# Splitting the last undivided product of a Strassen-Winograd kernel, and letting VectorE and GpSimd share its sums by turns

## The chip, the cores and the metric

The kernel runs on one core of one Trainium2 chip. The core has a matrix engine (TensorE, PE in the profile; its weight loads are a row of their own, PEld), a vector engine (VectorE, DVE), a scalar engine (ScalarE, ACT), a general engine (GpSimd, POOL) and a queue that issues transfers (SyncE, SP). The metric is device time in microseconds (us) of one execution; smaller is better.

## The reference

Every one of 64 sequences of 64 tokens (width 1024, float32) passes two residual layers.

```
# layer 0: a low-rank adapter, chosen per sequence
x = x + (x @ B0[id0].T) @ A0[id0].T            # rank 16
# layer 1: a dense product, and a gated mixture of low-rank experts
logits = x @ Wr.T + 5.0 * one_hot(id1)          # 8 experts
gates  = softmax over the two largest logits, 0 elsewhere
y = x @ W.T + 2.0 * sum_e gates[e] * (x @ A1[e].T) @ B1[e].T
out = x + y
```

W is 1024 x 1024. That dense product over 4096 tokens is the bulk of the work, all of it in float32.

## The kernel before

**Tiling.** The data lie transposed: the width on 128 partitions in eight chunks, tokens along the free axis. Tokens come in eight blocks of 512. Two blocks make a super-block `s` (0 to 3), and in each super-block the dense product `(W + I) x` is one 2 x 2 block product in Winograd's form of Strassen's scheme: seven *outer* products `n`, run in `ORDER` 1, 2, 6, 7, 5, 3, 4, instead of eight. Each outer product is done in the same way again: seven *inner* products `k`, in which the weight tile is 256 x 256 and the tokens 256 wide. In super-blocks 1 to 3 some inner products are divided a third time into seven *fine* products of 128 x 128 weights and 128 tokens: `k = 2` always, `k = 4` for the `n` in `FOURTH`.

**What a division costs besides the matmuls.** A divided product needs sums and differences of the operands' quarters first, and its results must be added up after. Weight sums depend on W alone, so super-block 0 makes them and stores them in DRAM (`s_kept`, and `f_kept` for the fine ones, made in super-block 1); later super-blocks load them.

- `outer` (line 688) makes the four sums of W's quarters for the outer products 5, 7, 6, 3, on DVE.
- `weights` (line 709) makes in super-block 0, for every `n`, the four inner sums 5, 6, 7, 3 out of `n`'s quarters, on Pool, and stores all seven tiles with SP; later it loads them. Its tiles come from the pool of slots `"s"`, 27 of them.
- `fine_weights` (line 746) makes the four sums for a fine product (on Pool, one step) or loads them.
- `inner_tokens` (line 800) makes four differences of token quarters (`k` = 5, 6, 7, 4): on DVE in super-block 0, on Pool later. `begin_fine` (line 979) makes the tokens' sums for a fine product, on Pool, one step.
- `token_sum` (line 778) makes the outer sums of tokens, on DVE.
- `product` (line 918) issues the matmuls of an inner product: four calls of 256 columns, plus two where the expert term is added. A float32 call shows as two passes in the trace.
- `leave` (line 951) evacuates PSUM: a copy by ACT where nothing is to be added, otherwise an addition by DVE (PSUM plus an SBUF tile).
- `fine_product` (line 995) issues the fine matmuls in four parts. ACT copies the parts out (`copy`), and `rest_` adds them on Pool with three instructions.
- `whole_product` (line 889) is used for the pairs `(s, n)` in `WHOLE`, here only (0, 1): the outer product 1 of super-block 0 is not divided. It runs 4 x 4 calls of 512 columns, with four copies by ACT.

**The rest of the work.** Per block: the adapter of layer 0 (gathers of its rows by Pool, `turn`, `project`, `adapt`, whose results DVE adds to x), the rows of the experts (`rows`), the gates (`gates`: some twenty small DVE instructions in a chain), and `weigh`. In PSUM eight banks are given out as four "l", two "a" and two "b".

**The order.** Nothing is issued as written. Every step goes to `plan.add` with the engines that may run it and the time it is thought to take there, what it reads and writes, a due time `at` (one inner product is one unit, a super-block 49), the slots it takes, and `sb=True` where it reads SBUF with both operands. `Plan.order` (line 65) then plays the kernel through: again and again it takes the engine on which something can start first, and on it the step of lowest `at` among those within 0.2 us. The starts found order the instructions of each engine and each queue. Real waits are on data alone. Where steps marked `sb` run on DVE and Pool at once, `PACE` slows both in the plan (to 0.36 and 0.73 of their speed). This is the loop's core:

```
            e = min(can, key=lambda e: min(can[e]))
            t0 = min(can[e])[0]
            _, n, t = min((steps[n]["at"], n, t) for t, n in can[e] if t <= t0 + self.LOOK)
```

`products` (line 859) orders a super-block: `begin` adds the sums of an outer product one product ahead, `step` one inner product with its evacuation, and `advance` the next part of every fine product under way.

Of the kernel before, what the change touches and what calls it, by code (L numbers as in the profile page):

```python
# [14 lines left out]
P = 128  # L15
# [18 lines left out]
class Plan:  # L34
# [14 lines left out]
    AHEAD = 6.0  # L49
    PACE = {"DVE": 0.36, "POOL": 0.73}  # L50
    SET = {"SP": 1.2, "DVE": 3.1, "POOL": 2.9}

# [12 lines left out]
    def order(self):  # L65
# [34 lines left out]
        turn = {tag: 0 for tag in turns}  # L100
        clock, end, where, now = dict(self.SET), {}, {}, {}
        moved = 0.0
        done = []
# [4 lines left out]
        def start(n, e):  # L108
            st = steps[n]
            t = clock.get(e, 0.0)  # L110
            if st["kb"] and e == "SP":
                t = max(t, moved - self.AHEAD)
            for d in st["begun"]:
                t = max(t, steps[d]["start"] + 0.1)
            for d in st["dep"]:
                t = max(t, end[d] + (0.0 if where[d] == e and not steps[d]["kb"] else self.LAG))
            want = {}
            for tag, _ in st["take"]:
                want[tag] = want.get(tag, 0) + 1
            for tag, c in want.items():  # L120
                if len(free[tag]) < c or (tag not in self.shared and turns[tag][turn[tag]] != n):
                    return None
                t = max(t, sorted(free[tag])[c - 1] + self.LAG)
                if tag in self.shared:

                    for m in ready:
                        if sum(g == tag for g, _ in steps[m]["take"]) > c and steps[m]["at"] < st["at"] and data(m) <= t:
                            return None
            return t

        while ready:
# [7 lines left out]
            e = min(can, key=lambda e: min(can[e]))  # L139
            t0 = min(can[e])[0]  # L140
            _, n, t = min((steps[n]["at"], n, t) for t, n in can[e] if t <= t0 + self.LOOK)
            st = steps[n]
            ready.discard(n)
            clock[e] = t + st["eng"][e]
            other = {"DVE": "POOL", "POOL": "DVE"}.get(e)
            if st["sb"] and other in now and clock[other] > t and steps[now[other]]["sb"]:

                mine, theirs = st["eng"][e] / self.PACE[e], (clock[other] - t) / self.PACE[other]
                both = min(mine, theirs)
                clock[e] = t + both + (mine - both) * self.PACE[e]  # L150
                clock[other] = t + both + (theirs - both) * self.PACE[other]
                end[now[other]] = clock[other]
            now[e] = n
            end[n] = clock[e]
# [27 lines left out]
def kernel(  # L182
# [70 lines left out]

    WHOLE = {(0, 1)}

    FINE = 1
    FOURTH = (1, 2, 6, 7, 3)

    pe, dve = Pinned(tc, nc.tensor), Pinned(tc, nc.vector)
# [3 lines left out]
    slots = {  # L263
        "q": 7, "s": 27, "tt": 3, "cp": 3, "t5": 2, "t6": 2, "t7": 2, "t4": 2, "o": 3, "hg": 3, "hd": 3,
        "gb": 2, "ga": 1, "bt": 1, "bx": 1, "h": 1, "l": 4, "a": 2, "b": 2,
# [205 lines left out]
    def adapt(k, h, at):  # L471
# [33 lines left out]
        for gi in range(NG):  # L505
            xs = part(x, gs=[gi])
            plan.add({"DVE": 0.62}, out(gi), [(px[gi],)] + xs, xs, at - 2 + 1.5 * gi * (k == 0))

# [157 lines left out]
    s_kept = tc.dram_tile([7, 7, P, QC * QO], F32, name="s_kept")  # L666
    f_kept = tc.dram_tile([7, 2, P, QC * QO], F32, name="f_kept")

    def fine_of(s, n):

        return ((2, 4) if n in FOURTH and (s, n) != (NSUP - 1, ORDER[-1]) else (2,)) if s >= FINE else ()

# [11 lines left out]

    DVE = {"DVE": 0.62}
    POOL = {"POOL": 1.25}

    def outer(n, at):

        if n == 5:  # L690
            m_q[5] = {k: ("m5",) + k for k in quarter[1, 0]}
            for k in m_q[5]:
                combine(m_q[5][k], quarter[1, 0][k], quarter[1, 1][k], ALU.add, at, DVE)
        elif n == 7:
            m_q[7] = quarter[1, 0]
            for k in m_q[7]:
                combine(m_q[7][k], quarter[0, 0][k], m_q[7][k], ALU.subtract, at, DVE)
        elif n == 6:
            m_q[6] = quarter[0, 0]
            for k in m_q[6]:  # L700
                combine(m_q[6][k], m_q[5][k], m_q[6][k], ALU.subtract, at, DVE)
        elif n == 3:
            m_q[3] = quarter[0, 1]
            for k in m_q[3]:
                combine(m_q[3][k], m_q[3][k], m_q[6][k], ALU.subtract, at, DVE)

    wt, ti = {}, {}

    def weights(s, n, at):
# [17 lines left out]
        for k, (u, v, op) in {  # L727
# [7 lines left out]
            vv = m[v] if isinstance(v, tuple) else out[v]  # L735
            combine(out[k], uu, vv, op, at - 4, POOL)
        for k in ORDER:
# [8 lines left out]
    def fine_weights(s, n, k, a, at):  # L746

        t, kept = ("sf", s, n, k), f_kept[n - 1, k // 4]

        def blocks():  # L750
            made[t] = new("s", [P, QC, QO], f"sf_{s}_{n}{k}")
            return made[t].rearrange("p c (o w) -> p (c o) w", w=P)

# [3 lines left out]

        def sums(e):
            f, w4 = blocks(), made[a].rearrange("p c (o w) -> p (c o) w", w=P)
            a11, a21, a12, a22 = (w4[:, x] for x in range(4))  # L760
            v = engine[e]
            v.tensor_tensor(f[:, 0], a21, a22, ALU.add)
            v.tensor_tensor(f[:, 1], f[:, 0], a11, ALU.subtract)
            v.tensor_tensor(f[:, 2], a11, a21, ALU.subtract)
            v.tensor_tensor(f[:, 3], a12, f[:, 1], ALU.subtract)

# [3 lines left out]
        if s == FINE:  # L770
            plan.add({"POOL": 1.6}, sums, [(a,)], [(t,)], at - 3, [("s", t)], sb=True)
            plan.add({"SP": 0.1}, keep, [(t,)], [("fine", n, k)], at + 4, kb=256)
        else:
            plan.add({"SP": 0.1}, load, [("fine", n, k)], [(t,)], at - 6, [("s", t)], kb=256)
        wt[n]["fine", k] = t
# [24 lines left out]
    def inner_tokens(s, n, m, at):  # L800
# [7 lines left out]
        for k, u, v in ((5, (0, 1), (0, 0)), (6, (1, 1), 5), (7, (1, 1), (0, 1)), (4, (1, 0), 6)):  # L808
            t = ("ti", s, n, k)

            def fn(e, t=t, k=k, u=u, v=v):
# [5 lines left out]
            plan.add(  # L817
                POOL if s else DVE, fn, keys(*u) + vk, [(t,)], at - 5,
                [(f"t{k}", t)], sb=True,
# [39 lines left out]
    def products(s):  # L859
# [91 lines left out]
        def leave(n, ps, i, cs, js, more=False):  # L951
# [18 lines left out]
            if d == n and not fresh:  # L970
                reads.append((name(d, i), 0, 0))
            plan.add(
                {"ACT": 0.6} if src is None else DVE, fn, reads, qk(d, i, cs, js), at() - 4,
                [("o", name(d, i))] * fresh,
# [4 lines left out]
        def begin_fine(n, k):  # L979

            t, (tx, tk) = ("tt", s, n, k), ti[n][k]

            def fn(e):
                made[t] = new("tt", [P, 4, P], f"tt_{s}_{n}{k}")
                f, b, v = made[t], tx(), engine[e]
                b11, b21 = b[:, 0, :P], b[:, 1, :P]
                v.tensor_tensor(
                    f[:, :2], b[:, :, P:], b[:, 0, :].rearrange("p (h t) -> p h t", t=P), ALU.subtract
                )
                v.tensor_tensor(f[:, 2], f[:, 1], b11, ALU.add)  # L990
                v.tensor_tensor(f[:, 3], b21, f[:, 2], ALU.subtract)

            plan.add({"POOL": 1.7}, fn, tk, [(t,)], at() - 3, [("tt", t)], sb=True)

        def fine_product(n, k, part_):


            ps, cp, tag = ("pf", s, n, k), ("cp", s, n, k), "b" if k == 2 else "l"
            a, f, t, (tx, tk) = wt[n][k], wt[n]["fine", k], ("tt", s, n, k), ti[n][k]
            extra = hd[n][k] if n in (2, 3, 7, 4) and part_ == 3 else None  # L1000
            oh, row = {2: 0, 3: 0, 7: 1, 4: 1}.get(n), k // 4

# [28 lines left out]

            reads = [(a,), (f,), (t,)] + tk + ([("b1",), extra[1]] if extra is not None else [])
            plan.add(
# [14 lines left out]
            if part_ < 3:  # L1048
# [4 lines left out]
                return  # L1053
            leave(n, ps, row, ALL, (0,), True)
            region = qk(dest[n], row, ALL, (0,))

            def rest_(e):
                o, c, v = q(dest[n], row, ALL, (0,)), made[cp], engine[e]
                c11, c21, c2 = o[:, 0, :P], o[:, 1, :P], o[:, 1]
                v.tensor_tensor(c11, c11, c[:, 0], ALU.add)  # L1060
                v.tensor_tensor(c2, c2, c[:, 1:3].rearrange("p h t -> p (h t)"), ALU.add)
                v.tensor_tensor(c21, c21, c[:, 3], ALU.add)

            plan.add({"POOL": 1.7}, rest_, [(cp,)] + region, region, at() - 4, sb=True)
            done(n, row, ALL, (0,))

# [62 lines left out]
        def step(n, k):  # L1129
# [8 lines left out]
            if k in (1, 6, 5, 3):  # L1138
# [5 lines left out]
                if k == 5 and last(n):  # L1144
                    leave(n, ps, 0, ALL, (1,))
                if k == 5 and 4 in fine_of(s, n):
                    leave(n, ("pb2", s, n), 1, ALL, (0,), True)
# [24 lines left out]
        for n in ORDER:  # L1172
# [21 lines left out]
            else:  # L1194
# [10 lines left out]
                for k in (6, 7, 5):  # L1205
                    step(n, k)
                    if k == 7 and 4 in fine_of(s, n):
                        going.append([n, 4, 0])
                    advance()
                if 4 in fine_of(s, n):  # L1210
                    rest = [(n, 3)]
                    continue
            rest = [(n, 4), (n, 3)] if last(n) else [(n, 3), (n, 4)]
# [94 lines left out]
```

## Time and profile before

| | before |
|---|---|
| median of 3 runs | 516.18 us (515.77 to 516.62) |
| the profiled execution's own time | 517.08 us |
| its span, first to last instruction | 515.3 us |
| TensorE clock granted | 0.999 |
| PE busy | 501.1 us, 97% |
| DVE busy | 329.3 us, 64% |
| Pool busy | 318.7 us, 62% |
| ACT busy | 71.4 us, 14% |
| transfers | 108.69 MB, mean 211 GB/s |

The page of the profile gives busy time by engine, then the span in 40 slices of 12.9 us (each digit tenths of a slice), then the chain of work that ended last. A row of the trace names start, duration, engine, operation, and "written tile <- read tiles". The names that matter here: `pw` the PSUM of an undivided product, `pa` and `pb` those of inner products, `pf` of fine ones, `ph` of the experts' rows, `px`, `pb<-x,bt` and `pt` of the adapter; `w`, `m` and `s` tiles of weights (loaded, outer sums, inner sums), `sf` fine weight sums, `ti` and `t` inner and outer sums of tokens, `tt` fine ones; `u`, `v` and `o` collect results. All lines are that of one helper (L29), so tiles tell instructions apart.

### The profile page before, as it was taken

The numbers are of one execution on the slowest core, as the hardware profiler recorded it, in microseconds if no ns is written. First come the engines' busy times: TensorE is split into PE (matmuls) and PEld (weight loads), VectorE is DVE, ScalarE is ACT, GpSimd is POOL, SyncE is SP. The second block draws the span as 40 slices with busy tenths as digits, with TensorE's granted clock in tenths as the row PEclk, the third lists the DMA queues.
The fourth block names the chain that finished last, engine by engine and source line by source line (L and its number), as shares of the span: only waits on it lengthen the run. The fifth ranks groups of instructions, "written<-read, shape, count | busy, mean of one in ns | idle before, by whom it ended". The sixth has DMA issues, their size and how long they took to land.

```text
span 515.3 us, 9478 instructions
## 1 busy us (share of the span) xinstructions
PE 501.1 (97%) x3648; PEld 441.6 (86%) x3648; DVE 329.3 (64%) x589; ACT 71.4 (14%) x189; POOL 318.7 (62%) x405
## 2 busy tenths in 40 slices
PE   2999999999999999999999999999999999999997
PEld 2857988889889998899888999889889899998986
DVE  0689998987975275536985456463878526742833
ACT  1111100001001130012110121102301111111110
POOL 3063058095467686997958557972954755997811
PEclk9999999999999999999999999999999999999999
DMA  7999185799585303999577633981855754581023
GB/s 260 371 354 369 67 280 211 256 332 317 176 261 206 90 15 101 335 342 350 173 253 248 211 131 118 380 281 43 284 176 190 246 149 134 169 270 41 38 98 111
DMA packets 59452, 108.69 MB, mean 211 GB/s; under 512 B 5520, under 2 KB 11664, under 8 KB 59408
## 3 DMA queue, kind: packets, MB, share of 16 engines
q1 hardware_dynamic: 57104, 99.70, 56.7%
q0 software_dynamic: 2304, 8.39, 4.8%
q8 instruction: 29, 0.48, 0.4%
q14 instruction: 15, 0.12, 0.1%
HBM read 75.30 MB, written 32.77 MB: 210 GB/s over the span
## 4 chain that ended last, share of the span: by engine, by line
PE 97%; DMA 2%; DVE 0%; issue 0%; SPq 0%; POOL 0%
PE pa L29 39%; PE pb L29 23%; PE pf L29 15%; PE ph L29 12%; PE px L29 3%; PE pw L29 3%; DMA x<-in_xT 2%; PE pt L29 1%; PE pg L29 1%; DVE o L29 0%; SPq L29 0%; DVE bx L29 0%; POOL x L29 0%
## 5 line engine op out<-in xcount | busy, mean ns | idle before, releaser
L29 PE MATMUL pa<-ti,s 128*128 128x256 f32 x432 | 102.0, 380 | 0.0
L29 PEld LDWEIGHTS pa<-ti,s 128*128 128x128 f32 x432 | 79.2, 190 | 9.8 <-issue 0.2
L29 PE MATMUL pb<-ti,s 128*128 128x256 f32 x264 | 65.6, 380 | 0.0
L29 PE MATMUL ph<-a_sb,x 128*128 128x136 f32 x512 | 62.8, 279 | 0.2 <-issue 0.2
L29 PEld LDWEIGHTS ph<-a_sb,x 128*128 128x128 f32 x512 | 61.8, 190 | 1.1 <-issue 0.4
L29 ACT COPY cp<-pf 128x128 f32<-128x128 f32 (+1 forms) x108 | 32.2, 302 | 201.0 <-PE pf L29 189.1
L29 PEld LDWEIGHTS pb<-ti,s 128*128 128x128 f32 x264 | 48.6, 190 | 5.9
L29 PE MATMUL pa<-x,s 128*128 128x256 f32 x216 | 52.4, 380 | 0.0
L29 POOL TENSOR_TENSOR ti<-x,ti 128x512 f32<-128x512 f32 x24 | 32.2, 1340 | 27.7 <-PE pf L29 22.6
L29 POOL TENSOR_TENSOR o<-o,cp 128x128 f32<-128x128 f32 (+1 forms) x54 | 34.5, 651 | 20.9 <-DVE o L29 15.6
L29 DVE TENSOR_TENSOR x<-px,x 128x512 f32<-128x512 f32 x64 | 39.8, 683 | 10.8 <-PE px L29 10.7
L29 PEld LDWEIGHTS pa<-x,s 128*128 128x128 f32 x216 | 39.4, 190 | 4.9 <-issue 0.2
L29 PE MATMUL pf<-tt,sf 128*128 128x128 f32 x216 | 42.1, 278 | 0.0
L29 POOL TENSOR_TENSOR ti<-t 128x512 f32<-128x512 f32 x18 | 23.3, 1294 | 29.3 <-PE pa L29 16.8
L29 POOL TENSOR_TENSOR ti<-x 128x512 f32<-128x512 f32 x24 | 31.0, 1292 | 16.7 <-PE pb L29 11.2
L29 PE MATMUL pa<-t,s 128*128 128x256 f32 x168 | 41.2, 380 | 0.0
L29 PEld LDWEIGHTS pf<-tt,sf 128*128 128x128 f32 x216 | 35.5, 191 | 3.2 <-issue 0.8
L29 DVE TENSOR_TENSOR o<-pa,u 128x512 f32<-128x512 f32 x32 | 22.0, 687 | 22.2 <-PE pa L29 11.2
L29 POOL TENSOR_TENSOR s<-w,w 128x512 f32<-128x512 f32 x12 | 17.1, 1428 | 29.1 <-PE pa L29 13.2
L29 POOL TENSOR_TENSOR ti<-t,ti 128x512 f32<-128x512 f32 x18 | 25.3, 1404 | 15.7 <-PE pf L29 12.2
L29 PEld LDWEIGHTS pa<-t,s 128*128 128x128 f32 x168 | 30.8, 190 | 3.9 <-issue 0.2
L29 DVE TENSOR_TENSOR o<-pb,o 128x512 f32<-128x512 f32 x35 | 23.6, 688 | 8.7 <-ACT o L29 4.6
(150 smaller groups left out, 850.9 us busy)
## 6 DMA issues: line engine op xcount, KB each, us to landing
s<-s_kept SPq DMA_DIRECT2D x147, 256.0 KB, 3.9
x<-in_xT SPq DMA_DIRECT2D x15, 1024.0 KB, 6.8
out_T<-o SPq DMA_DIRECT2D x30, 512.0 KB, 3.2
s_kept<-s SPq DMA_DIRECT2D x28, 256.0 KB, 4.6
sf<-f_kept SPq DMA_DIRECT2D x24, 256.0 KB, 2.8
s_kept<-w SPq DMA_DIRECT2D x18, 256.0 KB, 5.6
w<-in_w SPq DMA_DIRECT2D x16, 256.0 KB, 7.5
f_kept<-sf SPq DMA_DIRECT2D x12, 256.0 KB, 3.3
```

Of the source, the lines that this page charges most:

```text
L29: return self._tc.keep_in_program_order(f(*args, **kwargs))
```

## The change

1. `WHOLE` becomes empty: outer product 1 of super-block 0 is divided into seven inner products like all others.
2. W's inner sums in super-block 0 (`weights`) and the inner token differences in super-blocks 1 to 3 (`inner_tokens`) may go to DVE or to Pool. The plan takes the engine on which the step can start first. Token differences of super-block 0 stay on DVE.
3. The plan lets only one step marked `sb` run at a time over DVE and Pool; `PACE` goes. Durations in the plan change: 0.62 to 0.65 (two SBUF operands) or 0.69 (one in PSUM), 1.25 to 1.3.
4. The sums for fine products become steps of their own (four for weights, three for tokens), with the same instructions. `rest_` adds with two instructions of 256 columns rather than three of 128, 256 and 128, each a step.
5. The fine product `k = 4` is begun after inner product 6, not 7. A third kind, `k = 3`, is written down but used for no `n` (`THIRD` is empty).
6. The pool `"s"` has 26 slots, not 27.

```diff
-    PACE = {"DVE": 0.36, "POOL": 0.73}
...
-        moved = 0.0
+        moved = shared_ = 0.0
...
-            return t
+            return (max(t, shared_), t) if st["sb"] else (t, t)
...
-            t0 = min(can[e])[0]
-            _, n, t = min((steps[n]["at"], n, t) for t, n in can[e] if t <= t0 + self.LOOK)
+            t0 = min(can[e])[0][0]
+            _, n, t = min((steps[n]["at"], n, t) for (t, _), n in can[e] if t <= t0 + self.LOOK)
...
             clock[e] = t + st["eng"][e]
-            other = {"DVE": "POOL", "POOL": "DVE"}.get(e)
-            if st["sb"] and other in now and clock[other] > t and steps[now[other]]["sb"]:
...
+            if st["sb"]:
+                shared_ = clock[e]
...
-    WHOLE = {(0, 1)}
+    WHOLE = set()
...
     FOURTH = (1, 2, 6, 7, 3)
+    THIRD = ()
...
-        "q": 7, "s": 27, "tt": 3, "cp": 3,
+        "q": 7, "s": 26, "tt": 3, "cp": 3,
...
-            combine(out[k], uu, vv, op, at - 4, POOL)
+            combine(out[k], uu, vv, op, at - 4, {"DVE": 0.65, "POOL": 1.3})
...
-            plan.add({"POOL": 1.6}, sums, [(a,)], [(t,)], at - 3, [("s", t)], sb=True)
+            for x in range(4):
+                plan.add(
+                    {"POOL": 0.48}, sums(x), [(a,)] + [(t, y) for y in range(x)], [(t, x)], at - 3,
+                    [("s", t)] * (x == 0), sb=True,
+                )
...
-                POOL if s else DVE, fn, keys(*u) + vk, [(t,)], at - 5,
+                {"DVE": 0.65, "POOL": 1.3} if s else DVE, fn, keys(*u) + vk, [(t,)], at - 5,
...
-                c11, c21, c2 = o[:, 0, :P], o[:, 1, :P], o[:, 1]
-                v.tensor_tensor(c11, c11, c[:, 0], ALU.add)
-                v.tensor_tensor(c2, c2, c[:, 1:3].rearrange("p h t -> p (h t)"), ALU.add)
-                v.tensor_tensor(c21, c21, c[:, 3], ALU.add)
+                    o, c = (o[:, :, :P], c[:, 0::3]) if x == 0 else (o[:, 1].rearrange("p (h t) -> p h t", t=P), c[:, 1:3])
+                    v.tensor_tensor(o, o, c, ALU.add)
...
+            for x in range(2):
+                plan.add({"POOL": 0.75}, rest_(x), [(cp,)] + region, region, at() - 4, sb=True)
...
-                    if k == 7 and 4 in fine_of(s, n):
-                        going.append([n, 4, 0])
+                    if k in (6, 5) and k - 2 in fine_of(s, n):
+                        going.append([n, k - 2, 0])
```

## The prediction

> **What bounds the kernel now.** I read the page first: engine totals, then the 40 slices.
>
> ```profile
> PE 501.1 (97%) x3648; PEld 441.6 (86%) x3648; DVE 329.3 (64%) x589; ACT 71.4 (14%) x189; POOL 318.7 (62%) x405
> ...
> PE   2999999999999999999999999999999999999997
> ...
> DVE  0689998987975275536985456463878526742833
> ...
> POOL 3063058095467686997958557972954755997811
> ...
> PE 97%; DMA 2%; DVE 0%; issue 0%; SPq 0%; POOL 0%
> ```
>
> TensorE is busy in every slice but the first and the last, and the chain that ended last (the last line) is TensorE itself for 97%. So two things can move the time: less TensorE work, or a hole in it. Next, busy time by stage: the first super-block from 16 us, and the three later ones (columns: length, PE, PEld, DVE, ACT, POOL, clock, DMA).
>
> ```profile
> 16.00:102.00 86.00, 85.66 (x620) 69.48 (x620) 78.63 (x145) 8.74 (x18) 33.16 (x25) 1.00 0.76 268
> 131.00:254.00 123.00, 123.00 (x919) 110.29 (x921) 75.03 (x135) 18.75 (x50) 94.10 (x132) 1.00 0.60 205
> 254.00:378.00 124.00, 123.99 (x948) 111.31 (x944) 76.33 (x135) 20.01 (x56) 82.39 (x103) 1.00 0.62 211
> 378.00:502.00 124.00, 124.00 (x735) 112.37 (x728) 69.47 (x112) 18.36 (x55) 82.53 (x107) 1.00 0.48 153
> ```
>
> There is no hole to close: PE is busy 85.66 of 86 and 371 of 371. The tightness is in the first super-block, where DVE is busy 91% (78.63 of 86); later DVE stands at 56 to 62% and Pool at 66 to 77%. Now PE in order of time where the undivided product runs.
>
> ```profile
> 27.15 1.95 PE L29 MATMUL pb<-x,bt 128*32 128x128 f32 x64
> 29.03 3.70 PE L29 MATMUL pw<-x,w 128*128 128x512 f32 x8
> 32.66 1.17 PE L29 MATMUL px<-bx,ga 32*128 32x128 f32 x32
> 33.77 10.57 PE L29 MATMUL pw<-x,w 128*128 128x512 f32 x24
> ```
>
> Lengths overlap the next start by a drain, so I price by start to start: 3.63 (29.03 to 32.66) and 10.49 (33.77 to 44.26, the next px), 14.12 us. Last, DVE and Pool in order of time.
>
> ```profile
> 29.48 1.34 POOL L29 TENSOR_TENSOR s<-w,w 128x512 f32<-128x512 f32 x1 [9.97 <-DMA w<-in_w]
> 30.90 1.26 POOL L29 TENSOR_TENSOR s<-s,w 128x512 f32<-128x512 f32 x1
> ```
>
> ```profile
> 60.25 0.69 DVE L29 TENSOR_TENSOR ti<-t 128x512 f32<-128x512 f32 x1
> 60.86 0.69 DVE L29 TENSOR_TENSOR ti<-t,ti 128x512 f32<-128x512 f32 x1
> ...
> 63.98 0.69 DVE L29 TENSOR_TENSOR w<-m,w 128x512 f32<-128x512 f32 x1
> ...
> 74.08 1.75 DVE L29 TENSOR_TENSOR ti<-t 128x512 f32<-128x512 f32 x1
> 75.75 1.75 DVE L29 TENSOR_TENSOR ti<-t,ti 128x512 f32<-128x512 f32 x1
> ```
>
> DVE alone starts a sum every 0.60 us; against Pool the same sum lasts 1.75 and starts come 1.67 apart, while Pool's own sums (1.27 alone) lasted 1.71 at 73.56 and 75.24. One of each takes 1.67 where one after the other would take 1.87: they hardly overlap.
>
> **The change part by part.**
>
> *No undivided product.* Out go 32 passes over 512 columns, 14.12 us. In come seven inner products of eight 256-column passes. Such a product starts at 57.64 and the next at 59.37: 1.73 us, times seven 12.11. One more joint beside px costs about 0.1 (the product at 45.37 behind px takes 1.83 to the next start). Net −1.9 us, all on the path. Weight loads rise from 32 to 56 of 190 ns; PEld is busy 7.63 of 16 us between 29 and 45, and a pass takes 216 ns, so they stay beneath the matmuls. The page "TensorE: Matmul & The Clock Gate" (Back-to-back issue gap) says that small passes pay more per column, 262 cycles for 256 and 518 for 512; scaled so, seven products would be an estimated 12.5 us and the saving 1.6, and the rows above, which show 12.1, decide.
>
> DVE pays: four token subtractions for product 1 (4 × 0.60) and three evacuations that add (products 2, 5, 4; 3 × 0.60), 4.2 us. ACT copies four times before and after (586 ns each). About 1.4 us of the 4.2 fits the gap before 27.67, where DVE waited 1.43 us for the gate rows; 2.8 go into the full stretch. The W sums that PE now needs existed before: Pool began them at 29.48 and had the second at 32.16. PE needs them after two products and px, near 33.8. Cover 1.6 us; without it, 1.3 us per sum. The first W tiles' seven stores merely move up; DMA is full there (1.04 of its share), but the same stores stood at 33 to 44 already, behind the W loads. I take 0; bounds 0 to one 256 KB store, 0.7 us at 370 GB/s.
>
> *W's inner sums on DVE or Pool (super-block 0).* 28 sums: 1.27 on Pool or 0.60 on DVE. During the first gates, Pool's eight sums stretched DVE's gate chain from 4.6 us (the second block, 55.67 to 60.25, Pool idle) to 12.6 (27.67 to 40.31). Each sum that DVE takes costs it 0.60 and saves up to 1.0 of such waiting; between 60 and 70, where Pool is idle and DVE full, it is 0.60 lost. For eight such sums the bounds are −3.2 to +4.8 us of DVE time. I take 0, since both situations occur.
>
> *Later tokens' sums on DVE or Pool.* 28 per super-block at 1.27 on Pool; with half moved, DVE gains 14 × 0.60 = 8.4 us (61 to 68%) and Pool loses 18. Hidden by PE in all three rows above. If it is not, an evacuation stands behind a sum that waits for Pool: 1.75 in place of 0.69, 1.06 late. PE leaves 1.73 between product 6 and product 5 on the same bank, the evacuation takes 0.69: margin 1.04, nothing to spare with hand-over. I take 0; bounds −0.2 (all holes that PE shows) and +0.2 on each of 42 moved sums, 8.
>
> "SBUF — State Buffer" (Who interferes with whom) states an exclusive lock: a DVE sum with two SBUF inputs and a Pool instruction that reads SBUF exclude one another for the whole instruction. The 1.67 us per pair nearly agrees; by the rule a pair costs an estimated 1.87. It speaks against the wish to have both work: a sum on the free engine stops the other, and only moving it to the faster one frees time.
>
> *The plan's turns.* Steps with two SBUF inputs no longer overlap in the plan; durations go from 0.62 to 0.65/0.69 and 1.25 to 1.3. No instruction is added, but all queues, SP's and Pool's gathers among them, get a new order. Its only measure is PE's holes: gain at most 0.2 us, loss open. I take 0 beside the +8 above.
>
> *Fine products.* Sums split into single steps: same instructions. The rest adds go from three (578 + 798 + 578 ns) to two (2 × 798): 0.35 less for Pool, 36 times, 12.8 us, off the path. Product 4's fine passes start after product 6 rather than 7, 1.73 earlier: a PSUM bank is taken 1.73 longer, and product 5 gets 0.88 more distance from 6. Same PE work, 0; bounds ±0.5.
>
> *26 slots for W tiles.* Pool waited 5.9 us at 70.66 for a tile's store, and PE did not notice. With one fewer, a sum comes a store later (5.6 us to land). I take 0, upper bound in the first rival.
>
> Sum: −1.9. The profiled execution took 517.08 (span 515.3 and 1.78 around it), 0.90 above the median of 516.18. So 515.2 on its scale, 514.3 on that of the runs. What this measurement can tell from no change is 0.2%, 1.0 us.
>
> **The rivals.**
>
> *DVE comes too late in super-block 0 (slower).* W's first quarter for product 6 is ready at 64.67 and PE starts on it at 65.00: 0.33 to spare. PE will be there 1.9 earlier, DVE has 2.8 more and only 0.8 of idle before that (0.26 at 45.2, 0.52 at 48): 1.9 + 2.0 − 0.33 = 3.6 us of hole, net +1.7, 517.9. With 4.8 for W sums on DVE as well, net +6.5, 522.7. Against it: two products of outer product 2 (2.6 each, ordered between and behind) can be put ahead and fill 5.2. It decides from a hole of 1.9 on.
>
> *Evacuations behind blocked sums in the later super-blocks.* If one in three of 42 moved sums makes PE wait 0.15, that is 2.1 and the gain is gone: 516.4. For it: DVE carries more, with the margin of 1.04 above. Against it: contended sums on DVE at 74 to 77 already occur, and PE shows no gap.
>
> *The saving is not there:* small passes cost as much as large ones, 516.2. Against it: 216 ns for 256 columns and 437 for 512.
>
> **How the numbers follow.** PE stays fed, 513.8 to 515.1: 0.51. Holes give back about the gain, by either of the last two rivals, 515.2 to 517.2: 0.15. DVE late in super-block 0, 517.2 to 522.7: 0.21. Later holes of more than 3 us: 0.13. Thus faster 0.51, same 0.15, slower 0.34; the likeliest has 514.3 with 513.8 to 515.1 for itself. The upper end is put at 520.0, where about 0.1 is left out; the lower at 513.7, since nothing but 0.2 us of holes and 0.5 of order could add to the 1.9.
>
> **What would show it.** PE busy falls by 1.9, rows named pw vanish, 256-column rows gain 56 passes, and PE's length in the later super-blocks stays 124. DVE's busy time rises and Pool's falls by about 30 or more. Wrong if PE shows idle time with DVE or Pool as its releaser: between 44 and 82 us for the first rival, behind evacuations after 130 for the second.

## The result, and the profile after

The changed kernel takes 518.09 us (median of 8 runs, 517.3 to 519.1); the kernel before, run beside it, takes 516.50 (515.77 to 517.33). The ratio is 1.0031 [1.0017, 1.0044]: slower, by 0.9 to 2.3 us. The profiled execution took 517.92 us, with a span of 516.1.

The page of the changed kernel, engine totals, slices and the chain that ended last:

```profile
PE 498.7 (97%) x3672; PEld 446.1 (86%) x3672; DVE 343.2 (66%) x624; ACT 71.5 (14%) x189; POOL 279.9 (54%) x341
...
PE   2999899999999999999999999999999999999997
...
DVE  0798998988885467647885457553777627653843
...
POOL 3073036066257767887268376563855545677511
...
PE 90%; DVE 6%; DMA 2%; issue 1%; ACT 0%; DVEq 0%
```

Two things changed. PE has less to do (498.7 us against 501.1), and DVE has entered the chain with 6%, where it had 0%. One digit of PE's row has fallen from 9 to 8, the fifth, which is 52 to 64 us. DVE rose by 14 us and Pool fell by 39, as forecast.

Busy time by stage (length, PE, PEld, DVE, ACT, POOL, clock, DMA share, GB/s):

```profile
29.00:45.00 16.00, 14.98 (x143) 13.17 (x142) 15.59 (x30) 1.37 (x3) 12.98 (x11) 1.00 1.03 362
45.00:60.00 15.00, 14.76 (x80) 13.32 (x81) 13.45 (x38) 3.22 (x7) 0.00 (x0) 1.00 0.47 181
60.00:75.00 15.00, 13.28 (x66) 11.55 (x65) 14.76 (x23) 1.07 (x2) 3.38 (x3) 1.00 0.60 209
...
131.00:254.00 123.00, 123.00 (x921) 110.29 (x920) 82.18 (x146) 18.38 (x50) 82.77 (x113) 1.00 0.60 209
254.00:378.00 124.00, 124.00 (x941) 111.51 (x944) 75.33 (x139) 20.08 (x56) 73.59 (x86) 1.00 0.63 208
378.00:502.00 124.00, 124.00 (x755) 112.49 (x755) 75.17 (x123) 18.37 (x55) 71.99 (x84) 1.00 0.47 156
```

The later super-blocks are full, to the last digit. All that PE lost stands in the first three rows: 1.02 + 0.24 + 1.72 = 2.98 us. In the kernel before, PE was full in these three:

```profile
29.00:45.00 16.00, 16.00 (x92) 7.63 (x92) 15.69 (x29) 2.55 (x5) 11.23 (x9) 1.00 1.04 359
45.00:60.00 15.00, 15.00 (x115) 14.04 (x112) 13.52 (x38) 1.56 (x4) 1.88 (x2) 1.00 0.58 216
60.00:75.00 15.00, 15.00 (x76) 13.03 (x75) 14.83 (x22) 1.56 (x3) 5.32 (x4) 1.00 0.65 224
```

Who it waited for in the changed kernel (waits of PE: total, times, longest):

```profile
PE pa L29 <- DVE o L29: 1.7, 1, 1.7
PE pg L29 <- DVE h L29: 1.3, 1, 1.3
```

Both are VectorE. PE in order of time around the two places, and DVE there:

```profile
38.26 5.72 PE L29 MATMUL ph<-a_sb,x 128*128 128x136 f32 x48
45.24 0.63 PE L29 MATMUL pg<-ident,h 128*128 128x128 f32 x4 [1.26 <-DVE h L29]
...
61.81 1.04 PE L29 MATMUL pt<-ident,gb 128*128 128x128 f32 x8
64.57 1.99 PE L29 MATMUL pa<-ti,s 128*128 128x256 f32 x8 [1.72 <-DVE o L29]
```

```profile
38.39 2.68 DVE L29 TENSOR_TENSOR w<-w,ident 128x128 f32<-128x128 f32 x4
40.99 1.84 DVE L29 TENSOR_SCALAR den<-ex 128x4 f32<-128x4 f32 x1
...
44.41 0.68 DVE L29 TENSOR_TENSOR h<-h,s 128x512 f32<-128x512 f32 x1
...
60.83 0.68 DVE L29 TENSOR_TENSOR u<-pb,u 128x512 f32<-128x512 f32 x1
61.43 2.48 DVE L29 TENSOR_TENSOR m<-w,w 128x512 f32<-128x512 f32 x4
63.83 0.68 DVE L29 TENSOR_TENSOR o<-pa,u 128x512 f32<-128x512 f32 x1
```

First hole: the weighted rows `h` end at 45.09, because the gates' chain before them was held up. An instruction on 128 x 4 values (`den`) stood for 1.84 us, while Pool ran a gather (40.46 to 41.49) and a sum (41.52 to 42.80). That wait alone is longer than the hole, but it is not all that holds the chain up. From its first step to `h` the chain takes 17.3 us here (27.14 to 44.41) and took 12.6 before. DVE's waits inside it while Pool works are no longer than before: by an estimate from its rows, less what the same steps take where Pool makes no sums, 6.0 us here and 7.3 before. New inside it are eight additions of `px`, which came after `h` before, and two evacuations of the divided product, 6.0 us in all. Second hole: PE's next product waits for the evacuation `o<-pa` at 63.83, and ahead of that DVE had four outer sums of W, 2.48 us.

**A measure for comparing profiles.** The matmuls start when a gather and the first tokens have landed, and this varies: the first product began at 29.03 us in one profile of the kernel before and at 28.05 in another. So I also give, for each profile, the time from the first matmul of the first outer product (`pw<-x,w` or `pa<-x,w`) to the end of the span: *the body*. It is 486.27 and 486.15 for the two profiles before. For the changed kernel it is 516.1 − 28.50 = 487.6.

### The profile page after: what moved, and what is told of

Same layout as the page of the kernel before. It is cut to its first block, busy times and chain, and to the rows that moved or that the text cites. A ratio compares the mean times of both kernels' runs of the same rounds, so it can differ in the third digit from the quotient of the medians.

```text
span 516.1 us, 9516 instructions
## 1 busy us (share of the span) xinstructions
PE 498.7 (97%) x3672; PEld 446.1 (86%) x3672; DVE 343.2 (66%) x624; ACT 71.5 (14%) x189; POOL 279.9 (54%) x341
## 4 chain that ended last, share of the span: by engine, by line
PE 90%; DVE 6%; DMA 2%; issue 1%; ACT 0%; DVEq 0%
PE pa L29 39%; PE pb L29 22%; PE pf L29 15%; PE ph L29 10%; PE px L29 3%; PE pt L29 1%; DMA gb<-in_b,idx 1%; DVE x L29 1%; DVE t L29 1%; DVE w L29 1%; PE pg L29 1%; DVE c L29 0%; DVE m L29 0%; DVE u L29 0%; DVE den L29 0%
## 5 line engine op out<-in xcount | busy, mean ns | idle before, releaser
L29 PE MATMUL pa<-ti,s 128*128 128x256 f32 x448 | 106.5, 381 | 1.7 <-DVE o L29 1.7
L29 PEld LDWEIGHTS pa<-ti,s 128*128 128x128 f32 x448 | 81.8, 190 | 12.0 <-DVE o L29 2.0
L29 PE MATMUL pb<-ti,s 128*128 128x256 f32 x272 | 67.5, 380 | 0.0
L29 PE MATMUL pa<-x,s 128*128 128x256 f32 x224 | 54.4, 380 | 0.0
L29 POOL TENSOR_TENSOR o<-o,cp 128x256 f32<-128x256 f32 x36 | 33.3, 925 | 36.2 <-DVE o L29 19.3
L29 POOL TENSOR_TENSOR ti<-x,ti 128x512 f32<-128x512 f32 x22 | 28.5, 1293 | 22.3 <-PE pf L29 11.1
L29 PEld LDWEIGHTS pf<-tt,sf 128*128 128x128 f32 x216 | 36.2, 191 | 3.5 <-issue 0.6
L29 POOL TENSOR_TENSOR ti<-x 128x512 f32<-128x512 f32 x17 | 22.1, 1302 | 28.9 <-PE pb L29 21.9
L29 POOL TENSOR_TENSOR ti<-t,ti 128x512 f32<-128x512 f32 x12 | 15.6, 1298 | 16.2 <-DVE ti L29 8.4
L29 POOL DMA_INDIRECT gb<-in_b,idx x8 | 8.0, 1001 | 28.3 <-PE pt L29 24.6
L29 DVE TENSOR_TENSOR v<-pa,u 128x512 f32<-128x512 f32 x16 | 11.0, 687 | 17.3 <-PE pa L29 15.4
```

The lines of the kernel that those rows point to most:

```text
L29: return self._tc.keep_in_program_order(f(*args, **kwargs))
```

## The experiments

The main theory after the result (A) was that VectorE comes too late in super-block 0. It has two forms: the order of its steps is bad there (A1), or there is not enough time there in any order (A2). The rival (B) was that the rest of the change (the turns, the sharing) costs time by itself.

### Only the undivided product goes

```diff
-    WHOLE = {(0, 1)}
+    WHOLE = set()
```

Nothing else of the change is made.

> The kernel before with one edit: outer product 1 of super-block 0 is divided; plan, costs, engines and slots stay as before. Theory A (VectorE is short in super-block 0 once this product is divided): holes on TensorE between 38 and 66 us of 3 to 5 us, against 2 us less matmul work, so 517.5 to 519.5 beside 516.5 before; nothing changes after 130 us. Theory B (the new order by turns and the shared sums cost the time, the divided product alone saves it): no hole, 514.3 to 515.

Measured: 519.34 us beside 515.99, ratio 1.0067 [1.0053, 1.0082]; body 489.6. PE in order of time, then stretches of 1 us (columns as above):

```profile
60.94 1.04 PE L29 MATMUL pt<-ident,gb 128*128 128x128 f32 x8
64.56 3.50 PE L29 MATMUL pa<-ti,s 128*128 128x256 f32 x8 [2.57 <-DVE o L29]
```

```profile
65.00:66.00 1.00, 1.00 (x4) 0.82 (x3) 0.96 (x3) 0.00 (x0) 0.00 (x0) 0.50 0.70 70
```

The same evacuation is late again, behind the same four sums (61.41 to 63.90). The hole is 2.57 us, and after it the product of eight passes takes 3.50 us where it takes 1.99 in the changed kernel: the granted clock was 0.50 from 65 to 68 us and 0.85 in the next one, about 1.7 us lost. A further 0.9 hides inside a row: the second `px`, 1.2 us elsewhere, takes 2.10, since its banks came free late: DVE empties those of the first `px` only from 40.63 to 43.10. The hole behind `h` isn't there. Saving −1.6 (below) + 2.57 + 1.7 + 0.9 = +3.6; the body grew by 3.4. So the undivided product's removal alone makes the first super-block lose time, without any sharing or turns.

### All but the undivided product

```diff
-    WHOLE = set()
+    WHOLE = {(0, 1)}
```

in the changed kernel.

> The changed kernel with one edit: outer product 1 of super-block 0 is whole again; everything else of the change stays. Theory A: the holes at 44 and 63 us go, the 2 us of matmul work come back: 516.0 to 517.0, as before. Theory B: the loss of the rest shows without the saving, 519 to 520.5.

Measured: 519.14 beside 515.99, ratio 1.0063 [1.0049, 1.0077]; body 488.9. I had priced the rest at nothing, and it costs 3.1 us. DVE and Pool in order of time:

```profile
76.68 1.23 POOL L29 DMA_INDIRECT gb<-in_b,idx  x1
...
77.60 4.59 DVE L29 TENSOR_TENSOR ti<-t,ti 128x512 f32<-128x512 f32 x1
77.93 1.27 POOL L29 TENSOR_TENSOR s<-w,w 128x512 f32<-128x512 f32 x1
...
79.15 1.27 POOL L29 TENSOR_TENSOR s<-w,s 128x512 f32<-128x512 f32 x1
...
80.38 1.25 POOL L29 TENSOR_TENSOR s<-m,m 128x512 f32<-128x512 f32 x1
81.71 1.61 POOL L29 TENSOR_TENSOR s<-s,m 128x512 f32<-128x512 f32 x1
```

One token difference of 0.6 us lasted 4.59. Pool began three sums in that time, each as the one before ended; DVE got in at the first pause, between 81.63 and 81.71. The evacuations behind it came late: a hole of 1.82 us at 81.1 to 82.9, with no drop of the clock. The second `px` took 2.28 instead of 1.2. Together 2.9; the body grew by 2.7.

So both halves lose, +3.3 and +3.1 us, and together only +1.6: in the changed kernel the order avoids the long wait (no single DVE instruction lasts more than 2.1 us there).

### The four sums later

```diff
-                outer(5, at() + 4)
+                outer(5, at() + 7)
```

in the changed kernel: the sums that stand ahead of the late evacuation are due three products later.

> The changed kernel with one edit: the four outer weight sums m5 are due three units later (at + 7, not at + 4), so that they need not stand ahead of the evacuation that TensorE waited for at 62.8 us. Theory A1 (the hole there is a matter of order on VectorE: 2.5 us of sums ahead of one evacuation): the 1.7 us hole shrinks by 1 us or more, 516.5 to 517.3. Theory A2 (VectorE simply has too much work up to there, whatever its order): the hole moves a few us on and keeps its size, 517.8 to 518.5.

Measured: 518.27 beside 515.99, ratio 1.0048 [1.0034, 1.0062]; body 487.8. The hole behind the evacuation shrank from 1.7 to 0.9, a new one of 0.4 appeared behind another DVE step, the first stayed at 1.27: 2.55 in all against 2.98, and no time gained (PE also waits 0.26 for a load of x at 106 us). The hole shrank almost as A1 asked, the time is the one of A2. A better place for these four sums gains nothing, which speaks for A2 without settling it.

### Token differences of super-block 0 on either engine

```diff
-                {"DVE": 0.65, "POOL": 1.3} if s else DVE, fn, keys(*u) + vk, [(t,)], at - 5,
+                {"DVE": 0.65, "POOL": 1.3}, fn, keys(*u) + vk, [(t,)], at - 5,
```

in the changed kernel: if DVE is short of time, Pool can take some.

> The changed kernel with one edit: the inner token differences of super-block 0 may also go to Pool, which stands idle from 43 to 63 us. If what is short is VectorE's own time, Pool relieves it by 0.6 us for each and the hole goes: 515.5 to 517. If what is short is the time in which one of the two may read two operands from SBUF, each difference costs 1.27 on Pool in place of 0.60, and the hole stays or grows: 518.1 to 520.

Measured: 525.87 beside 515.99, ratio 1.0185 [1.0164, 1.0207]; body 496.5. That is far above what either theory gave. Waits of PE:

```profile
PE ph L29 <- DVE x L29: 3.3, 1, 3.3
PE pa L29 <- DVE s L29: 2.5, 1, 2.5
PE pa L29 <- DVE o L29: 1.5, 2, 0.8
```

DVE was given less and came later: 13.40 us busy between 29 and 45 against 15.59, and PE waited 7.3 us for it (after the two largest holes, with the clock at 0.50 as well). A sum on Pool keeps DVE's two-input instructions out for 1.27 us, where DVE would have been done in 0.60. The Trainium skill has the rule on "SBUF — State Buffer" (Who interferes with whom): a VectorE instruction with two SBUF inputs and a GpSimd instruction that reads SBUF lock each other out for the whole instruction; these waits agree with it. Before the largest hole one addition of the identity lasts 3.27 us on DVE, from 36.2 us on, while Pool ends a gather and runs two of the moved differences. So what is short in super-block 0 seems to be the two engines' common time, of which Pool makes poor use; how much of the loss is Pool's longer sums and how much such waits, this run doesn't separate.

### W's sums on Pool alone, with the rest of the change

```diff
-            combine(out[k], uu, vv, op, at - 4, {"DVE": 0.65, "POOL": 1.3})
+            combine(out[k], uu, vv, op, at - 4, {"POOL": 1.3})
```

in the kernel with all but the undivided product.

> The second experiment (the changed kernel with outer product 1 of super-block 0 whole) with one edit more: W's inner sums in super-block 0 go to Pool alone again. In the second experiment TensorE stood still for 1.8 us behind a VectorE sum of super-block 0 that lasted 4.59 us while Pool ran its sums of W one after the other. Theory C (sharing W's inner sums sets the two engines against each other in super-block 0): the hole goes, 516 to 517. Theory D (the plan by turns and its new durations make that order, whoever does W's sums): the hole stays, 518.5 to 519.5.

Measured: 518.58 beside 516.48, ratio 1.0043 [1.003, 1.0056]; body 487.8. The hole at 81 us is gone, as C said, but the time is D's. The body grew by 1.6: the second `px` takes 2.26 instead of 1.2, and PE waits 0.7 us at 145. That wait is for an evacuation that itself waited for a store of the output. PE and DVE there:

```profile
145.68 1.99 PE L29 MATMUL pa<-ti,s 128*128 128x256 f32 x8 [0.72 <-DVE o L29]
```

```profile
144.93 0.69 DVE L29 TENSOR_TENSOR o<-pa,u 128x512 f32<-128x512 f32 x1 [1.40 <-DMA out_T<-o]
```

Pool shut DVE out here too, at 116.12 for 3.27 us, again after a gather (114.09), though no wait of PE follows from it. Sharing W's sums is therefore not needed for it; the next experiment looks at the order.

### The plan's turns alone

```diff
-            return t
+            return (max(t, shared_), t) if st["sb"] else (t, t)
...
+            if st["sb"]:
+                shared_ = clock[e]
```

in the kernel before, without `PACE`; no step changes its engine or its duration in the plan.

> The kernel before with one edit: the plan lets the two engines into SBUF by turns; durations, engines, slots and the whole product stay. Theory C: no hole, 515.5 to 516.5. Theory D: a hole of 1 to 3 us between 60 and 90 us, 517.5 to 519.

Measured: 521.34 beside 516.48, ratio 1.0103 [1.0073, 1.0133]; body 490.9. That is more than either theory gave: measured alone, the costliest part of the change is the one without an instruction. DVE and Pool in order of time, then PE:

```profile
75.43 0.96 POOL L29 DMA_INDIRECT gb<-in_b,idx  x1 [0.87 <-PE pt L29]
...
75.96 5.93 DVE L29 TENSOR_TENSOR x<-x,x 128x512 f32<-128x512 f32 x1
76.41 1.28 POOL L29 TENSOR_TENSOR s<-s,w 128x512 f32<-128x512 f32 x1
...
77.64 1.26 POOL L29 TENSOR_TENSOR s<-w,w 128x512 f32<-128x512 f32 x1
...
78.86 1.26 POOL L29 TENSOR_TENSOR s<-w,s 128x512 f32<-128x512 f32 x1
80.08 1.25 POOL L29 TENSOR_TENSOR s<-m,m 128x512 f32<-128x512 f32 x1
81.41 1.60 POOL L29 TENSOR_TENSOR s<-s,m 128x512 f32<-128x512 f32 x1
```

```profile
82.64 3.65 PE L29 MATMUL pa<-t,s 128*128 128x256 f32 x8 [2.30 <-DVE u L29]
```

The new order puts a gather just ahead of W's sums on Pool. Four of them pass a waiting DVE sum, 5.93 us; PE then waits 2.30, and the clock falls to 0.50 for three microseconds: the product after the hole takes 3.65 instead of 1.89. 2.3 + 1.7 = 4.0 of the 4.7 us by which the body grew.

### The changed kernel with less for VectorE

```diff
+        if (s, n) == (0, 1):
+            out.update({k: (("view", i, j), keys(i, j)) for k, i, j in ((5, 0, 1), (6, 1, 1), (7, 1, 1), (4, 1, 0))})
...
+            if (s, n) == (0, 1):
+                continue
...
-    for i in range(4):
-        add_identity(i, -30)
```

The four token differences of outer product 1 and the eight identity additions are left out (inner products 4 to 7 then read plain quarters of x, and W goes without I, so the output is another): the same work for PE, and less for DVE. I reckoned with 5.7 us less; in the trace DVE is busy 336.5 us, 6.7 less than in the changed kernel.

> The changed kernel with VectorE work of super-block 0 left out: the four inner token differences of outer product 1 (their products read undivided quarters in their place) and the eight additions of the identity to W's diagonal blocks, about 5.7 us of VectorE; the matmuls are the same in number and shape, so the output is not the reference's. Theory A (VectorE short in super-block 0, the saving on TensorE real): no hole over 0.5 us and 514 to 515.3. If the holes are a matter of waits or of order, they stay, 517.5 to 518.5.

Measured: 515.68 beside 516.48, ratio 0.9985 [0.9976, 0.9993]. The profiled execution took 514.16, and PE was full from 29 us to 502; body 484.1, which is 2.1 less than before. So the saving exists, and with less work for DVE in super-block 0 the holes that eat it are gone. The plan orders this kernel anew as well, so the order may have a share in that. But the median fell by 0.8 only. Two further profiles of this kernel were to show where the rest went.

> The changed kernel less 5.7 us of VectorE's work (the four token differences of product 1 and the identity additions left out), profiled a second time, since its median was 0.8 us below the kernel before while its profile was 1.9 below. If the saving is real and executions only start later or earlier, TensorE is again full from 29 us on, and any difference in time stands before 29 us. If the late steps come back in some executions, holes appear between 44 and 90 us.

> As the second profile of this kernel: full from 29 us on with the difference before 29 us, or holes between 44 and 90 us.

Measured: 516.31 and 514.70; bodies 485.8 and 484.8. PE of the first of these two, around the second `px`:

```profile
33.82 1.97 PE L29 MATMUL pa<-x,s 128*128 128x256 f32 x8
35.72 2.58 PE L29 MATMUL px<-bx,ga 32*128 32x128 f32 x32
38.23 1.99 PE L29 MATMUL pb<-x,s 128*128 128x256 f32 x8
```

This `px` takes 1.28 in the profile of 514.16 us, 1.88 in that of 514.70, and 2.58 here; little else differs after the start (484.1 + 0.6 and + 1.3 come within 0.4 of the other two bodies). PE's gaps show 0.3 us of it at most. The 32 matmuls wait bank by bank for DVE: inside the row they stand still until 35.93, 36.55 and 37.14, each about 0.05 us after the end of one of DVE's additions of the `px` before (35.89, 36.49, 37.09). In this profile Pool began W's sums, when a tile of W landed, at 27.85, into the gates' chain. That is 0.9 us before the first product of the body; it was 0.2 before it in the profile of 514.70, and 0.5 behind it (28.65) in that of 514.16. So how late DVE is at 36 us goes with when W's tiles land, and even with less work it is late in some executions.

### The changed kernel profiled again

> The changed kernel, unchanged, profiled a second time. If the holes are a property of the order, VectorE's two late steps (h near 45 us and product 6's evacuation near 64 us) are there again, 2.5 to 3.2 us in all between 29 and 75 us. If they depend on the moment, they lie elsewhere or differ by more than 0.5 us. The first matmul's wait for the gathered rows shows whether the 10.2 us of the first profile belongs to the change or varies (9.1 to 10.1 in the other kernels).

> As the second profile of the changed kernel: the same two holes, 2.5 to 3.2 us between 29 and 75 us, and a start that varies; or holes elsewhere.

Measured: 517.59 and 517.72; bodies 487.3 and 487.6. The second hole is the same in all three profiles (1.72, 1.73, 1.73), the first is 1.26, 0.85, 1.26. In the one with 0.85 `den` took 0.16 us and the wait fell on the step after next, 1.64 us. The first matmul of all came 0.2 to 0.3 us earlier than in the first profile (10.2 us). Less their holes (2.98, 2.58, 2.98 between 29 and 75 us) the three bodies are 484.6, 484.7 and 484.6: 1.6 us below the 486.2 before.

### Undoing the long wait in two ways

The kernel before, unchanged, was profiled again as well:

> The kernel before once more, unchanged, for a second profile: the first was taken in an execution of 517.08 us, over the median of its runs. Expected: TensorE full from 16 us on, as in the first, a span of 514 to 515.5, the difference before 16 us, where transfers decide.

515.98 us, PE full from 29 us on, body 486.15.

With the plan's turns alone, the gather is held back until W's last inner sum of outer product 5 (the first) or two of W's sums change places, so that a sum that needs the one before it comes earlier (the second):

```diff
-            behind=[(("x", 0, 1), 0, 0)] * ((tag, k) == ("ga", 0)) + [("a1",)] * (k == 1) + [(("px", 1, 1, 0),)] * (k > 1),
+            behind=[(("x", 0, 1), 0, 0)] * ((tag, k) == ("ga", 0)) + [("a1",)] * (k == 1) + [(("px", 1, 1, 0),)] * (k > 1) + [(("s", 0, 5, 3),)] * ((tag, k) == ("gb", 4)),
```

```diff
+            3: ((0, 1), 6, ALU.subtract),
             7: ((0, 0), (1, 0), ALU.subtract),
-            3: ((0, 1), 6, ALU.subtract),
```

> The sixth experiment (the kernel before with the plan by turns) with one edit: the fifth block's gather of adapter rows waits in Pool's order until the last inner sum of W for outer product 5 has begun, so that no gather stands among Pool's sums between 70 and 85 us. In the sixth run a VectorE sum issued just behind that gather waited 5.93 us for SBUF. Theory E (Pool's sums shut VectorE out where they follow a gather without a gap): the long wait and the 2.3 us hole go, 516 to 517. Theory F (it is the plan by turns, wherever the gather stands): a hole stays, 519 to 522.

> The sixth experiment with another edit: in each outer product Pool makes W's inner sums in the order 5, 6, 3, 7 in place of 5, 6, 7, 3, so that 6 and 3 both need the sum just ahead of them and Pool pauses before each. In the traces VectorE came in at such a pause of 0.08 us. Theory G (VectorE gets SBUF only at a pause of Pool): the wait of 5.93 us shortens to two sums of Pool, 2.5 to 3.2 us, and the time falls to 517.5 to 519.5. If a pause makes no difference, 521 again.

Measured: 516.65 and 516.62 beside 516.18, ratios 1.0011 [0.9998, 1.0023] and 1.0013 [1.0003, 1.0022]; bodies 486.7 and 486.8. Either one removes 4 us of the 4.7. In the second the gather stays where it was; DVE and Pool there:

```profile
75.07 0.96 POOL L29 DMA_INDIRECT gb<-in_b,idx  x1 [0.85 <-DMA s_kept<-s]
...
75.62 2.26 DVE L29 TENSOR_TENSOR x<-x,x 128x512 f32<-128x512 f32 x1
76.04 1.28 POOL L29 TENSOR_TENSOR s<-s,w 128x512 f32<-128x512 f32 x1
77.40 1.61 POOL L29 TENSOR_TENSOR s<-w,s 128x512 f32<-128x512 f32 x1
```

Pool's second sum now needs the first, starts 0.08 us after it, and DVE enters in that pause: 2.26 in place of 5.93. This was better than I had expected (517.5 to 519.5).

The gather held back in the kernel with all but the undivided product, and there also `THIRD = (1,)`, a third fine product for outer product 1:

> The second experiment (the changed kernel with the undivided product back) with the gather moved behind Pool's sums as in the ninth. If the whole loss of the rest of the change (3.1 us) came from VectorE shut out once at 77.6 us, 516 to 517; if new durations, sharing or the later super-blocks cost something as well, 517.5 to 519.

> The eleventh with THIRD = (1,): in super-blocks 1 to 3 the inner product 3 of outer product 1 is done as a fine product too, seven small products for eight, which saves TensorE 1.73 - 1.54 = 0.19 us three times. If nothing else moves, 0.6 us below the eleventh, at best 515.5; if its extra sums or its loads make a hole, above it.

Measured: 516.88 and 516.20 beside 516.18, ratios 1.0020 [1.0008, 1.0032] and 1.0006 [0.9997, 1.0014]; bodies 486.7 and 486.1. The long wait was most of the rest's loss: without it 0.7 of 3.1 us remains. The second `px` still takes 2.26 there, 1.1 more than before, which is more than the 0.5 by which the body grew. The extra fine product gives 0.7 (0.6 expected) and brings the kernel level with the one before, not below. No version that computes everything is faster than the kernel before.

## Why the prediction was wrong

**The saving: right.** I took −1.9. The bodies less their holes give −1.6, and the kernel with less for DVE −2.1 in its best profile. From start to start, all inner products take 279.35 us in the changed kernel and 267.21 before: dividing added the 12.1 us of my rows, and some 0.4 us are `px`, `pt` and other short products that take longer. The Trainium skill's page "TensorE: Matmul & The Clock Gate" (Back-to-back issue gap) gave an estimate of 12.5 us and a saving of 1.6, which meets the bodies but not the products' own time. Rows named `pw` are gone and there are 24 more passes (56 of 256 columns for 32 of 512). The third rival, that the saving is not there, is refuted.

**VectorE's share in super-block 0: the step that failed.** I priced it (four differences and three evacuations, 4.2 us, of which 2.8 go "into the full stretch") and then let it cost nothing in the likeliest case, "PE stays fed", on the ground that two products could be put ahead. That had 0.51. The first rival, with 0.21, is what happened: for it I worked out a hole of 3.6 and a net of +1.7, 517.9 us; measured are holes of 2.6 to 3.0 and +1.6, 518.1 us. The signs were in the places I named, DVE as PE's releaser between 44 and 82 us. The tile was not: I expected W's quarters for product 6 to be late, and it was the gates' `h` and an evacuation behind W's sums. So the nearness of the two sums is in part luck. The reserve of two products did not help: PE waited for `h` and, at the second hole, for a PSUM bank that DVE had yet to empty. My own rule said that a hole of 1.9 decides; with DVE at 91% and 2.8 us to place, the chance of such a hole should have been the larger one.

**W's inner sums: taken as 0 between −3.2 and +4.8.** Not separable in the changed kernel. My price of the waiting in the first gates was too high. The 4.6 us of the undisturbed chain run to the end of `h` and the 12.6 to its start; to the start of `h` they are 4.0 and 12.6. Of the 12.6, about 1.4 us are six additions of the identity and one `bx`, which the undisturbed chain has not, and an estimated 7.3 are waits while Pool works. In the changed kernel the waits in the chain are an estimated 6.0 us; with the additions of `px` and the evacuations ahead of `h` they are now on the path and make the first hole. The cover of 1.6 us for the first sums held: no product waited for W at 33.8.

**Later tokens' sums: right at 0.** PE is at 123.00, 124.00 and 124.00. Evacuations behind blocked sums cost nothing there; the second rival is refuted.

**The plan's turns: wrong at 0.** "Its only measure is PE's holes" was true, and the loss was left open without a size. Alone it is +4.9 us, 4 of them through one blocked DVE sum. It did not add up in the changed kernel, since the other parts gave another order. The parts measured one at a time (+3.3, +3.1) say nothing about their sum (+1.6): every part reorders every queue.

**Fine products, slots.** In the later super-blocks nothing is lost with them. What is left of the rest's cost when the long wait is undone, 0.7 us, shows as DVE late for the second `px` in super-block 0; which part of the rest makes it so is open. The 26 slots weren't tried by themselves.

## What to carry to other kernels

Where a helper engine is at 91% in the one stage that has no slack, work added to it there is on the path until the profile shows the gap that it fits into; price it as a hole first, and ask what the average hides second. Give work to the free one of two engines only if they don't exclude one another: here each sum moved to Pool took twice DVE's time out of both. And a planner's rule without an instruction can be the costliest line of a diff; measure it alone, but don't add up parts that each reorder everything.

## What the runs showed of the hardware

**Turns between VectorE and GpSimd are not fair.** I had counted on one wait of at most one sum: 1.75 us, as in two rows of the profile before. That profile holds a longer one, which the prediction doesn't mention and which cost PE nothing:

```profile
253.87 2.39 DVE L29 TENSOR_TENSOR o<-v,o 128x512 f32<-128x512 f32 x1
```

A waiting DVE instruction was passed by three and by four Pool sums in a row (4.59 and 5.93 us) as long as each followed the other without a pause, and got in at the first pause of 0.08 us. The Trainium skill's page "SBUF — State Buffer" (Who interferes with whom) tells who blocks whom by who issues first, which these rows do not follow: DVE's instruction at 75.96 was there before the Pool sums of 77.64, 78.86 and 80.08. A pause isn't always needed: at 74.08 and 75.75 in the kernel before, DVE and Pool alternate sum by sum without one, and the wait of 3.27 us in the kernel with W's sums on Pool alone ended without one. All single DVE instructions above 2 us in these runs (5.93, 4.59, twice 3.27, the 2.39 and some of 2.1 to 2.3) began during a gather by Pool or within 1.1 us of its end, and moving the gather removed the first two. Why the gather matters was not shown.

**In these runs a hole of more than two microseconds cost more than itself.** After holes of 2.30, 2.55, 2.57 and 3.34 us the granted clock was 0.50 for 3.4 us each time, 1.7 us of work lost; after 1.72, 1.73 and 1.82 it stayed at 1.00. "TensorE: Matmul & The Clock Gate" (Why this matters for your kernels) asks for no gaps above about 3 us; here the drop came already at 2.3. Four against three cases don't fix a limit.

**A wait can hide inside a row.** Thirty-two `px` matmuls show as one row of 1.28, 1.88 or 2.58 us, with next to no idle time named: they wait bank by bank for DVE's additions. Where a row is longer than its like elsewhere, the starts of its single instructions show whether it holds a wait.
